# First attention loads in halves, a backlog in the planner, second block's tokens normalised earlier, key differences stored from ScalarE

## The chip, the cores and the metric

The kernel runs on one core of one Trainium2 chip. The time is device microseconds (us) of one execution. The kernel before was timed three times; its median is 1596.62 us (1595.55 to 1596.75).

## The reference

One adaLN transformer block on `x` of shape (2, 1024, 512), all in float32:

```python
mod = (silu(c) @ wmod).reshape(2, 6, 1, 512)      # sa, ca, ga, sb, cb, gb
h = layernorm(x) * (1 + ca) + sa
q, k, v = h @ Wq, h @ Wk, h @ Wv                  # 32 query heads, 8 key heads, 64 wide
q, k = rope(q), rope(k)
attn = softmax(causal(q @ k.T / 8)) @ v           # 4 query heads share a key head
x = x + ga * (attn @ Wo)
h = layernorm(x) * (1 + cb) + sb
gate, up = split(h @ ternary(w_gate_up).T)        # 2048 hidden
x = x + gb * (rmsnorm(silu(gate) * up) @ ternary(w_proj).T)
```

`ternary` replaces each group of 64 weights by -1, 0 or 1 times the mean of their absolute values.

## The kernel before

Products that need float32 accuracy are made of two parts: a value is rounded to `F32R` (the "H" tile, by ScalarE) and what is left over is the "L" tile (`V.tensor_tensor(..., ALU.subtract)` on VectorE). A product is then H·H + L·H + H·L, which is three times the matmuls.

**Stage one, about 0 to 260 us.** The 2048 tokens are four blocks of 512. Each block goes through `keys_values(blk)` and then, for blocks 0 to 2, `queries(blk, g)` for the eight head groups `g`. The order of instructions on each engine is the order of the Python text. `queries` does, for one group: 24 matmuls into two PSUM tiles `pqk` (`rope_mm`); for block 0 the split of another part of Wq (`split_w`, which makes `wqH` on ScalarE and `wqL` on VectorE); four VectorE products with cosine and sine (`ra`, `rc`, `rb`, `rd`, in `rope_mul`) and two sums on GpSimd; and in `rope_end(1)` the split of the group before into `rr`, which SyncE stores to `qs` in DRAM (`put_q`, four transfers of 256 KB). In between, the next block is prepared: `stats` and `rstd` (mean, and the power -1/2 on GpSimd, tile `rs`), `norm` (VectorE, in place in `xt`, two calls in each of the groups 0 and 1), `first_T` (TensorE transposes, tile `pt`, groups 2 to 5) and `first_h` (tiles `h`, `hH`, `hL`).

Keys are stored twice: as values (`ks`), and as differences of keys 128 apart (`kds`, the tiles `ra` and `rc` with their float32r rounding from ScalarE). The SyncE queue issues every transfer of the kernel, in order. Each transfer waits for its source and for the transfer eight before it.

**From block 3's queries on** a planner (`Plan.run`) writes the order. Every step is a task with an engine, an estimated cost, a due time `due`, the tasks it needs, and the buffers and PSUM banks that it takes. The planner keeps its own clock and takes the available task with the smallest due time; its result is a fixed order of instructions for each engine. `moving` is its idea of when the transfers issued so far will have landed, and it starts at 0. The tasks are: 16 halves of the last block's queries (`mm`, 12 matmuls each), attention, the output projection, the second norm, ternary weights (spread between the other stages, the first from `TBEG` before the projection) and the feed-forward.

Attention goes by units: 2 batches x 8 head groups x 4 strips of 256 query rows. For a unit, the row maxima are needed first: `top_mm` (tile `pm`, TensorE), `top_red` (VectorE, tiles `mm` and `mx`), then four small transfers `row<-mt`. The scores (`ps_`), the exponentials (`e`, ScalarE), the weighted values (`po`) and the row sums (`pr`) follow. Tops are due `LEAD` before the unit's scores. `STICK` favours tasks of the kind that TensorE is at, and `FEED`, `BOOST`, `ENOUGH` and `DELAY` move `top_mm` forward or back by how much VectorE has left to reduce.

The first unit of a head group loads its keys: `k1` and `k2` (`load_k`, four transfers of 256 KB), the differences `k3` (`load_steps`, four) and for every second group the values `vt` (`load_v`, 512 KB). Each unit also loads its queries `t` (512 KB). The tiles `rr` of the last queries have two buffers, freed when their four stores have landed:

```python
        ha = add("A", ac(512, 0), due + 8, lambda hi=hi: hi(0, "ra"), (ja,), takes=("rr",))
        w = [add("S", 0.46, due + 11, lambda put=put, h=h: put(h), (la, lc), dma=256 * KB) for h in (0, 2, 1, 3)]
        ha.hold("rr", *w)
```

Of the kernel before, what the change touches and what calls it, by code (L numbers as in the profile page):

```python
# [61 lines left out]
class Plan:  # L62
# [39 lines left out]
    def run(self):  # L102
        wait, then, ready = {}, {}, {}
        for t in self.tasks:
            deps = {d.n: d for d in t.after + t.before}
            wait[t.n] = len(deps)
            for d in deps.values():
                then.setdefault(d.n, []).append(t)
            if not deps:
                ready.setdefault(t.eng, []).append((0.0, t))  # L110
        free, moving, ring, mode, port, left = {}, 0.0, 0.0, 0, 0.0, len(self.tasks)
        rows, owed = [0.0, 0.0], 0.0
        while left:
            best = self.order = None
            for eng, ts in ready.items():
                opts = []
                for r, t in ts:
                    at = self.room(t)
                    if at is not None:
                        now = free.get(eng, 0.0) if eng != "T" else max(rows) if t.lane is None else rows[t.lane]  # L120
                        r = max(r, at, port if eng == "P" or t.mode and eng == "V" else 0.0)
                        opts.append((max(r, now), r > now - AHEAD * (eng == "T"), t))
                if not opts:
                    continue
                start = min(o[0] for o in opts)
# [12 lines left out]
            ready[t.eng] = [o for o in ready[t.eng] if o[1] is not t]  # L138
            self.given = []
            for tag in t.takes:  # L140
                if tag[0] == "#":
                    self.given.append(self.order[len(self.given)][1])
                    self.banks[self.given[-1]] = lambda t=t, tag=tag: t.users[tag]
                else:
                    self.slots[tag].append(lambda t=t, tag=tag: t.users[tag])
            t.emit()
            owed += t.feeds
            if t.eng == "T":
                if t.mode != mode:
                    start = max(start, *rows) + (LEAVE if mode == 0 else ENTER)  # L150
                    rows, mode = [start, start], t.mode
                elif late and t.lane is None:
                    start += LOAD
                t.done = start + t.cost
                if t.lane is None:
                    rows = [t.done, t.done]
                else:
                    rows[t.lane] = t.done
            else:
                free[t.eng] = t.done = start + t.cost  # L160
            if t.eng == "P" or t.mode and t.eng == "V":
                port = t.done + 0.06
            if t.eng is None:
                free[None] = t.done = 0.0
            if t.dma:
                ring = max(start + (0.26 if t.eng == "A" else 0.03), ring) + t.cost
                free[t.eng] = ring
                moving = max(ring + 0.7, moving) + t.dma / 250e3
                t.done = moving + 0.95
            for d in then.get(t.n, ()):  # L170
                wait[d.n] -= 1
                if not wait[d.n]:
                    r = max([a.done + (self.LAG if a.eng != d.eng or a.dma else 0.1) + (SPARE if a.dma and d.eng != "S" else 0.0) for a in d.after], default=0.0)
                    ready.setdefault(d.eng, []).append((r, d))
# [3 lines left out]
EB, EL = 4, 10  # L178
SPAN = {2: 2, 4: 4, 6: 3, 8: 4}
HELD = 4  # L180
TBEG, TEND, PER_UNIT = 300, 20.0, 0.8
VSUM, VSIGN, LAST = 9, 1, 3
TBEFORE, TGAP, TSKIP = 20, 20.0, 25.0
LEAD, SPREAD, STICK, LATE = 15, 0.6, 9, 4
ENTER, LEAVE, LOAD, AHEAD = 0.16, 0.37, 0.1, 0.25
CLASS = (0, 1, 1, 2)
TURN, SPARE = 0.05, 1.0
FEED, BOOST, ENOUGH, DELAY, FILL = 0.3, 22, 2, 8, 3.5
QT, PACE = 6, 4

@with_exitstack
def block_kernel(ctx, tc, x, wq, wk, wv, wo, wgu, wpj, cin, wmod, cos, sin, out):
# [190 lines left out]
    first = {}  # L383
# [77 lines left out]
    def rope_end(n):  # L461
        while len(ropes) > n:
            (a, c, *steps), tok, dst = ropes.pop(0)
            rr = tp.tile([128, 4, 512], F32R, name="rr")
            for i, r in enumerate((a, c)):
# [10 lines left out]
                A.activation(high, steps[i], AF.Copy)  # L476
                V.tensor_tensor(rr[:, 2 + i, 128:512], steps[i], f32(high), ALU.subtract)
                half = [x for pair in kds for x in pair][[x for pair in ks for x in pair].index(dst)][i]
                SY.dma_start(f32(half[:, to:to + 512 - f]), f32(r[:, f:512].bitcast(F32R)))
            for h in (0, 2, 1, 3):  # L480
                if len(dst.shape) == 4:
                    put_q(dst, rr, h, tok)
# [37 lines left out]
    def queries(blk, g):  # L520
        rope_mm(blk, "wq", g * 256, qs[blk // 2][g])
        nxt = blk < 3 and 2 <= g < 6
        if nxt:
            first_T(blk + 1, g - 2)
        if blk == 0 and g < 4:
# [6 lines left out]
            mods_T(g - 1)  # L532
        if nxt:
            first_h(blk + 1, g - 2)
        if blk < 3 and g < 2:
            norm(blk + 1, 2 * g)
            norm(blk + 1, 2 * g + 1)
        rope_end(1)
# [239 lines left out]
    def attention(u):  # L778
# [15 lines left out]
        if u % NI == 0:  # L794
            kd = K[(b, g)] = {}

            def load_k(n):
                l, a = n // 2, n % 2
                if a == 0:
                    kd["k", l] = kp.tile([128, S], F32R, name=("k1", "k2")[l])  # L800
                SY.dma_start(f32(kd["k", l][a * 64:a * 64 + 64, :]), f32(ks[b][g // 4][l * 64:l * 64 + 64, g % 4, :]))

            def load_v():
                kd["vt"] = kp.tile([128, S // 128, 128], F32, name="vt")
                SY.dma_start(kd["vt"], vs[b * S:(b + 1) * S, g * 64:g * 64 + 128].rearrange("(t p) n -> p t n", p=128))

            kd["l"], before = [], K[units[u - 1][:2]]["l"] if u else []
            def load_steps(n):
                if n == 0:
                    kd["k", 2] = pp.tile([128, S // 8 * 7], F32R, name="k3", bufs=2)  # L810
                p = n % 2 * 64 + n // 2 * 32
                SY.dma_start(f32(kd["k", 2][p:p + 32, :]), f32(kds[b][g // 4][n // 2, g % 4 * 32:g % 4 * 32 + 32, :]))

            for n in range(4):
                kd["l"].append(add("S", 0.46, t0 - 26 + n, lambda n=n: load_k(n), order=kd["l"] + (held or before),
                                   takes=(("k1",), (), ("k2",), ())[n], dma=256 * KB))
            for n in range(4):
                kd["l"].append(add("S", 0.46, t0 - 22 + n, lambda n=n: load_steps(n), order=kd["l"], takes=() if n else ("k3",), dma=96 * KB))
            if g % 2 == 0:
                kd["lv"] = add("S", 0.46, t0 - 15, load_v, order=held or (K[units[u - 8][:2]]["lv"],) if u >= 8 else (), takes=("vt",), dma=512 * KB)  # L820
                kd["av"] = []
            else:
                kd["lv"] = K[(b, g - 1)]["lv"]
                kd["av"] = K[(b, g - 1)]["av"]
            kd["use"] = []

        kd = K[(b, g)]

# [40 lines left out]
        for n, (h0, s_, c, lo, hi) in enumerate(jobs):  # L869
            w = (hi - lo) * 128  # L870
            due = t0 - LEAD - pace * (len(jobs) - n)
            m = add("T", pe(w) + 0.03, due, lambda a=(h0, s_, c, lo, hi): top_mm(*a), d["lq"] + kd["l"][:2], takes=("#", "#1"), mode=3)
            tag = "mx" if hi == 2 * i + s_ + 1 else "mm"
            for n_, h in enumerate((h0, h0 + 2)):
                r = add("V", dv(w) + ((0.075 if c else 0.015) if tag == "mx" else 0.0), due + 0.01 * n_, lambda a=(h, s_, c, lo, hi): top_red(*a), (m,), order=[low[h, s_]] if c else (),
# [74 lines left out]
        for at, j in enumerate(order):  # L950
# [1 line left out]
            due = due_s[(u, j)]  # L952
            es[j] = []
            first, c = j in FIRST[nb], max(x for x in FIRST[nb] if x <= j)
            p = add("T", (3 + first) * pe(2 * n) + 0.03, due, lambda j=j: score(j), d["lq"] + kd["l"] + [row] + (cleared[1:2] if u == 0 else []) + ([] if first else es[j - 1]),
                    takes=("#", "#1") if first else (), mode=3)
            if first:
                chain[c] = p
# [15 lines left out]
            if (at + 1) % SPAN[nb] == 0:  # L974
                js = order[at + 1 - SPAN[nb]:at + 1]
                v = add("T", (SPAN[nb] * 2048 - (1024 if nb - 1 in js else 0)) / 2400 + 0.02, due + 5,
                        lambda js=js: [value(x) for x in js], sum((ex[x] for x in js), []) + [kd["lv"]], order=vals[-1:],
                        takes=("#",) if at == SPAN[nb] - 1 else (), mode=1)
                kd["av"].append(v)
                vals.append(v)  # L980
# [645 lines left out]
```

## Time and profile before

| | |
|---|---|
| median of three runs | 1596.62 us |
| profiled execution, its own time | 1598.2 us |
| its span, first to last instruction | 1596.3 us |
| TensorE (PE) busy | 1548.1 us, 97% |
| VectorE (DVE) busy | 1175.4 us, 74% |
| GpSimd (POOL) busy | 863.0 us, 54% |
| ScalarE (ACT) busy | 697.8 us, 44% |
| 16 transfer engines, q1 | 53.0% of their span |
| mean granted TensorE clock | 0.990 |

The profile is one execution of 1598.2 us, 1.6 us above the median, with 1.9 us outside the span. Busy shares are means over stages. TensorE is idle for 48 us in all, so what can be gained lies in where these are. A timeline line gives start, duration, engine, operation, tiles written and read, the count of merged instructions, and in brackets the idle time before and what ended it. `SPq` is SyncE's transfer queue. "L39" is the helper through which every instruction is recorded, so the tiles tell which step a line is.

### The profile page before, as it was taken

The numbers are of one execution on the slowest core, as the hardware profiler recorded it, in microseconds if no ns is written. First come the engines' busy times: TensorE is split into PE (matmuls) and PEld (weight loads), VectorE is DVE, ScalarE is ACT, GpSimd is POOL, SyncE is SP. The second block draws the span as 40 slices with busy tenths as digits, with TensorE's granted clock in tenths as the row PEclk, the third lists the DMA queues.
The fourth block names the chain that finished last, engine by engine and source line by source line (L and its number), as shares of the span: only waits on it lengthen the run. The fifth ranks groups of instructions, "written<-read, shape, count | busy, mean of one in ns | idle before, by whom it ended". The sixth has DMA issues, their size and how long they took to land.

```text
span 1596.3 us, 26757 instructions
## 1 busy us (share of the span) xinstructions
PE 1548.1 (97%) x9028; PEld 1068.0 (67%) x9028; DVE 1175.4 (74%) x2468; ACT 697.8 (44%) x1349; POOL 863.0 (54%) x758
## 2 busy tenths in 40 slices
PE   8899998989999999999999999999999999999998
PEld 7777887745555555555555555477788887888886
DVE  6888887778777788888878888857888674443444
ACT  3322222146555556555555656634655432222221
POOL 4364556537666765765676675713323544444343
PEclk9999999999999999999999999999999999999999
DMA  7775758775555546655646555576777833020000
GB/s 247 243 201 173 225 150 230 227 182 163 154 146 150 143 125 172 167 157 141 169 123 172 146 150 144 161 244 198 251 216 246 288 102 136 1 79 1 11 16 27
DMA packets 206592, 250.55 MB, mean 157 GB/s; under 512 B 34932, under 2 KB 144500, under 8 KB 206456
## 3 DMA queue, kind: packets, MB, share of 16 engines
q1 hardware_dynamic: 206456, 248.85, 53.0%
q8 instruction: 71, 1.16, 0.3%
q14 instruction: 65, 0.53, 0.1%
HBM read 156.24 MB, written 92.02 MB: 156 GB/s over the span
## 4 chain that ended last, share of the span: by engine, by line
PE 70%; DVE 13%; DMA 6%; issue 5%; SPq 3%; ACT 2%; POOL 1%; DVEq 0%; ACTq 0%; POOLq 0%
PE pgu L39 15%; PE po L39 13%; PE pj L39 10%; PE pfo L39 7%; PE pqk L39 6%; PE pm L39 5%; DVE junk L39 3%; SPq L39 3%; PE pr L39 2%; DVE rr L39 2%; DMA k<-ks 1%; DMA t<-qs 1%; DVE mm L39 1%; DVE ra L39 1%; DVE rd L39 1%
## 5 line engine op out<-in xcount | busy, mean ns | idle before, releaser
L39 POOL TENSOR_TENSOR acc<-acc,e 128x512 f32<-128x512 f32 x202 | 266.0, 1328 | 61.6 <-DVE acc L39 47.7
L39 PE MATMUL po<-e,vt 128*64 128x512 f32 (+1 forms) x1280 | 268.0, 557 | 4.2 <-DVE mx L39 1.6
L39 PE MATMUL pgu<-h,gu 128*128 128x512 f32 x1024 | 244.3, 391 | 0.0
L39 PEld LDWEIGHTS pgu<-h,gu 128*128 128x128 f32 x1024 | 192.0, 188 | 39.8
L39 DVE CUSTOM_DVE_ANT_0 junk<-pm,cmask,mm 128x384 bf16<-128x384 f32 (+1 forms) x256 | 174.6, 682 | 57.7 <-PE pm L39 33.2
L39 PEld LDWEIGHTS po<-e,vt 128*64 128x64 f32 x1280 | 84.0, 136 | 154.8 <-issue 123.3
L39 PE MATMUL pm<-k,t 64*128 64x384 f32 (+3 forms) x768 | 167.1, 384 | 16.1 <-DVE mx L39 6.0
L39 POOL TENSOR_SCALAR_AFFINE_SELECT e<-e 128x512 f32<-128x512 f32 x128 | 88.3, 692 | 143.6 <-ACT e L39 140.9
L39 PEld LDWEIGHTS pm<-k,t 64*128 64x128 f32 x768 | 93.5, 185 | 105.6 <-issue 31.6
L39 POOL TENSOR_TENSOR s<-hm 128x512 f32<-128x512 f32 x59 | 68.7, 1164 | 163.3 <-DVE hm L39 163.1
L39 DVE CUSTOM_DVE_ANT_0 junk<-pm,cmask 128x128 bf16<-128x128 f32 (+3 forms) x256 | 124.6, 487 | 41.4 <-PE pm L39 18.8
L39 DVE TENSOR_REDUCE mm<-pm 128x1 f32<-128x384 f32 (+2 forms) x256 | 128.3, 546 | 31.6 <-PE pm L39 31.1
L39 PE MATMUL pj<-woH,oh 128*128 128x512 f32 x512 | 142.2, 399 | 0.0
L39 POOL TENSOR_TENSOR on<-on,ri 128x512 f32<-128x512 f32 x64 | 85.5, 1337 | 66.8 <-DMA ri<-linv 62.7
L39 DVE TENSOR_TENSOR mL<-hm,mH 128x512 fp32r<-128x512 f32 x64 | 75.9, 1186 | 60.7 <-ACT mH L39 60.7
L39 DVE TENSOR_TENSOR hm<-gs,pgu 128x512 f32<-128x512 f32 x64 | 43.9, 686 | 94.3 <-PE pgu L39 89.9
L39 PEld LDWEIGHTS pj<-woH,oh 128*128 128x128 f32 x512 | 95.1, 188 | 20.9 <-issue 2.3
L39 ACT ACTIVATE mH<-hm 128x512 fp32r<-128x512 f32 x64 | 40.4, 632 | 146.1 <-PE pfo L39 133.3
L39 POOL TENSOR_TENSOR ra<-ra,rb 128x512 f32<-128x512 f32 x40 | 51.7, 1291 | 94.4 <-DVE rb L39 82.5
L39 PE MATMUL pfo<-pj,mH 128*128 128x512 f32 x256 | 100.4, 392 | 0.0
L39 PE MATMUL pfo<-pj,mL 128*128 128x512 f32 x256 | 99.7, 389 | 0.0
L39 POOL TENSOR_TENSOR sq<-sq,s 128x512 f32<-128x512 f32 x59 | 80.8, 1369 | 4.5
(1485 smaller groups left out, 3667.6 us busy)
## 6 DMA issues: line engine op xcount, KB each, us to landing
qs<-rr SPq DMA_DIRECT2D x128, 256.0 KB
t<-qs SPq DMA_DIRECT2D x64, 512.0 KB
k<-ks SPq DMA_DIRECT2D x64, 256.0 KB
ri<-linv SPq DMA_DIRECT2D x128, 128.0 KB
os<-on SPq DMA_DIRECT2D x64, 256.0 KB
ks<-rr SPq DMA_DIRECT2D x32, 256.0 KB
w<-in_wgu SPq DMA_DIRECT2D x32, 256.0 KB
gus<-wr SPq DMA_DIRECT2D x32, 256.0 KB
```

Source lines behind the costliest of these rows:

```text
L39: ins = f(*a, **k)
```

## The change

1. `Plan.run` starts `moving` at `BACKLOG` = 8 instead of 0.
2. For the first unit (`u == 0`), `k1`, `k2`, `k3` and `vt` are loaded in two halves each. The first halves keep their due times, the second halves are due from `TSECOND` = 30. Strips 0 and 1 need the first halves alone (`i > 1` adds the rest). That is nine more transfers on SyncE. The size that the planner assumes for a `k3` load goes from 96 to 112 KB.
3. In `queries(0, g)` for `g < 2`, `norm` is called ahead of `split_w`.
4. The stores into `kds` are issued by ScalarE instead of SyncE (16 of them).
5. `TBEG` 300 to 330, `LEAD` 15 to 11, `STICK` 9 to 6, `FEED` 0.3 to 0.6, `BOOST` 22 to 14, `ENOUGH` 2 to 3.

```diff
-        free, moving, ring, mode, port, left = {}, 0.0, 0.0, 0, 0.0, len(self.tasks)
+        free, moving, ring, mode, port, left = {}, BACKLOG, 0.0, 0, 0.0, len(self.tasks)
...
-TBEG, TEND, PER_UNIT = 300, 20.0, 0.8
+TBEG, TEND, PER_UNIT = 330, 20.0, 0.8
...
-LEAD, SPREAD, STICK, LATE = 15, 0.6, 9, 4
+LEAD, SPREAD, STICK, LATE = 11, 0.6, 6, 4
...
-FEED, BOOST, ENOUGH, DELAY, FILL = 0.3, 22, 2, 8, 3.5
+FEED, BOOST, ENOUGH, DELAY, FILL = 0.6, 14, 3, 8, 3.5
+TSECOND, BACKLOG = 30.0, 8.0
...
-                SY.dma_start(f32(half[:, to:to + 512 - f]), f32(r[:, f:512].bitcast(F32R)))
+                A.dma_start(f32(half[:, to:to + 512 - f]), f32(r[:, f:512].bitcast(F32R)))
...
+        if blk == 0 and g < 2:
+            norm(blk + 1, 2 * g)
+            norm(blk + 1, 2 * g + 1)
         if nxt:
             first_T(blk + 1, g - 2)
         if blk == 0 and g < 4:
...
-        if blk < 3 and g < 2:
+        if 0 < blk < 3 and g < 2:
             norm(blk + 1, 2 * g)
             norm(blk + 1, 2 * g + 1)
...
+            parts = 1 + (u == 0)
-            def load_k(n):
+            def load_k(n, part=0):
...
+                c = slice(part * S // parts, (part + 1) * S // parts)
+                SY.dma_start(f32(kd["k", l][a * 64:a * 64 + 64, c]), f32(ks[b][g // 4][l * 64:l * 64 + 64, g % 4, c]))
...
+            if parts == 2:
+                for f, n in [(load_k, 0), (load_k, 1)] + [(load_steps, n) for n in range(4)] + [(load_k, 2), (load_k, 3)]:
+                    kd["m"].append(add("S", 0.46, TSECOND + len(kd["m"]), lambda f=f, n=n: f(n, 1), order=kd["l"] + kd["m"] + [kd["lv"]], dma=(128 if f is load_k else 48) * KB))
+                kd["mv"].append(add("S", 0.46, TSECOND + 8, lambda: load_v(1), order=kd["m"], dma=256 * KB))
...
-            m = add("T", pe(w) + 0.03, due, lambda a=(h0, s_, c, lo, hi): top_mm(*a), d["lq"] + kd["l"][:2], takes=("#", "#1"), mode=3)
+            m = add("T", pe(w) + 0.03, due, lambda a=(h0, s_, c, lo, hi): top_mm(*a), d["lq"] + kd["l"][:2] + kd["m"][:2] * (i > 1), takes=("#", "#1"), mode=3)
```

In the order that results, the changes on TensorE up to the first scores are these: before, 5 query halves of the last block, then the first six `pm` matmuls; after, 8 query halves and then the same six. SyncE's queue at this place, before: nine loads of keys and values with two of `t`, then the stores `qs_0` and `qs_1`, then `row` of unit 0, `qs_2`, `qs_3`, `row` of unit 1, `qs_4`, and `t` of unit 2. After: nine first halves with the two `t`, nine second halves, then `qs_0` to `qs_2`, `row` of unit 0, `qs_3`, `qs_4`, `t` of unit 2, `row` of unit 1. VectorE's order in group 0 of block 0, before: `wqL`, `ra`, `rc`, `rb`, `rd`, `xt`, `xt`; after: `xt`, `xt`, `wqL`, `ra`, `rc`, `rb`, `rd`; and likewise in group 1, whose end has the two `rr` of group 0.

More of the change, by code (lines that the diff above doesn't have):

```diff
@@ L795, in attention @@
             kd = K[(b, g)] = {}
-            def load_k(n):
+            parts = 1 + (u == 0)
+            def load_k(n, part=0):
                 l, a = n // 2, n % 2
-                if a == 0:
+                if a == 0 and part == 0:
                     kd["k", l] = kp.tile([128, S], F32R, name=("k1", "k2")[l])
[L801 to L805, printed above, removed]
+                c = slice(part * S // parts, (part + 1) * S // parts)
+                SY.dma_start(f32(kd["k", l][a * 64:a * 64 + 64, c]), f32(ks[b][g // 4][l * 64:l * 64 + 64, g % 4, c]))
@@ L807, in attention, with load_v, load_steps @@
+            def load_v(part=0):
+                if part == 0:
+                    kd["vt"] = kp.tile([128, S // 128, 128], F32, name="vt")
+                c, r = (slice(part * n // parts, (part + 1) * n // parts) for n in (S // 128, S))
+                SY.dma_start(kd["vt"][:, c], vs[b * S:(b + 1) * S, g * 64:g * 64 + 128][r].rearrange("(t p) n -> p t n", p=128))
             kd["l"], before = [], K[units[u - 1][:2]]["l"] if u else []
-            def load_steps(n):
-                if n == 0:
+            def load_steps(n, part=0):
+                if n == 0 and part == 0:
@@ L810, in load_steps @@
                     kd["k", 2] = pp.tile([128, S // 8 * 7], F32R, name="k3", bufs=2)
                 p = n % 2 * 64 + n // 2 * 32
-                SY.dma_start(f32(kd["k", 2][p:p + 32, :]), f32(kds[b][g // 4][n // 2, g % 4 * 32:g % 4 * 32 + 32, :]))
+                c = (slice(0, S // 8 * 7), slice(0, 512), slice(512, S // 8 * 7))[parts - 1 + part]
+                SY.dma_start(f32(kd["k", 2][p:p + 32, c]), f32(kds[b][g // 4][n // 2, g % 4 * 32:g % 4 * 32 + 32, c]))
             for n in range(4):
@@ L815, in attention @@
                 kd["l"].append(add("S", 0.46, t0 - 26 + n, lambda n=n: load_k(n), order=kd["l"] + (held or before),
-                                   takes=(("k1",), (), ("k2",), ())[n], dma=256 * KB))
+                                   takes=(("k1",), (), ("k2",), ())[n], dma=256 * KB // parts))
             for n in range(4):
-                kd["l"].append(add("S", 0.46, t0 - 22 + n, lambda n=n: load_steps(n), order=kd["l"], takes=() if n else ("k3",), dma=96 * KB))
+                kd["l"].append(add("S", 0.46, t0 - 22 + n, lambda n=n: load_steps(n), order=kd["l"], takes=() if n else ("k3",), dma=112 * KB // parts))
@@ L819, in attention @@
             if g % 2 == 0:
-                kd["lv"] = add("S", 0.46, t0 - 15, load_v, order=held or (K[units[u - 8][:2]]["lv"],) if u >= 8 else (), takes=("vt",), dma=512 * KB)
+                kd["lv"] = add("S", 0.46, t0 - 15, load_v, order=held or (K[units[u - 8][:2]]["lv"],) if u >= 8 else (), takes=("vt",), dma=512 * KB // parts)
                 kd["av"] = []
@@ L825, in attention @@
             kd["use"] = []
+            kd["m"], kd["mv"] = [], K[(b, g - 1)]["mv"] if g % 2 else [kd["lv"]]
+            if parts == 2:
+                for f, n in [(load_k, 0), (load_k, 1)] + [(load_steps, n) for n in range(4)] + [(load_k, 2), (load_k, 3)]:
+                    kd["m"].append(add("S", 0.46, TSECOND + len(kd["m"]), lambda f=f, n=n: f(n, 1), order=kd["l"] + kd["m"] + [kd["lv"]], dma=(128 if f is load_k else 48) * KB))
+                kd["mv"].append(add("S", 0.46, TSECOND + 8, lambda: load_v(1), order=kd["m"], dma=256 * KB))
         kd = K[(b, g)]
@@ L954, in attention @@
             first, c = j in FIRST[nb], max(x for x in FIRST[nb] if x <= j)
-            p = add("T", (3 + first) * pe(2 * n) + 0.03, due, lambda j=j: score(j), d["lq"] + kd["l"] + [row] + (cleared[1:2] if u == 0 else []) + ([] if first else es[j - 1]),
+            p = add("T", (3 + first) * pe(2 * n) + 0.03, due, lambda j=j: score(j), d["lq"] + kd["l"] + kd["m"] * (i > 1) + [row] + (cleared[1:2] if u == 0 else []) + ([] if first else es[j - 1]),
                     takes=("#", "#1") if first else (), mode=3)
@@ L976, in attention @@
                 v = add("T", (SPAN[nb] * 2048 - (1024 if nb - 1 in js else 0)) / 2400 + 0.02, due + 5,
-                        lambda js=js: [value(x) for x in js], sum((ex[x] for x in js), []) + [kd["lv"]], order=vals[-1:],
+                        lambda js=js: [value(x) for x in js], sum((ex[x] for x in js), []) + (kd["mv"] if i > 1 else [kd["lv"]]), order=vals[-1:],
                         takes=("#",) if at == SPAN[nb] - 1 else (), mode=1)
```

## The prediction

> **What bounds the kernel now.** I read the busy shares first, then the waits of TensorE (PE), then windows of 5 us where PE is idle, then timelines of the engine that ends each wait. PE is busy for 97% of the span, so the 48 us that it is not are all there is to gain, plus what a reduced clock takes after a stall.
>
> ```profile
> PE 1548.1 (97%) x9028; PEld 1068.0 (67%) x9028; DVE 1175.4 (74%) x2468; ACT 697.8 (44%) x1349; POOL 863.0 (54%) x758
> PE pt L39 <- DVE xt L39: 6.0, 3, 4.3
> PE pm L39 <- DVE mx L39: 6.0, 19, 0.5
> PE pm L39 <- DMA t<-qs: 5.8, 2, 5.3
> ```
>
> In the waits (total, times, longest) two single waits stand out, and the change is aimed at both: `pt` on `xt` (4.3) and `pm` on the load of `t` (5.3). The rest are waits of half a microsecond on VectorE's maxima. The second one, in windows (PE, PEld, DVE, ACT, POOL busy, clock, transfers) and on PE's timeline:
>
> ```profile
> 270.00:275.00 5.00, 5.00 (x24) 3.98 (x22) 2.99 (x5) 1.00 (x2) 3.80 (x4) 1.00 1.01 292
> 275.00:280.00 5.00, 0.22 (x1) 0.00 (x0) 1.89 (x3) 0.89 (x2) 2.52 (x2) 0.91 1.05 221
> 280.00:285.00 5.00, 4.08 (x12) 3.14 (x13) 2.06 (x12) 0.00 (x0) 0.00 (x0) 0.50 1.09 249
> 280.49 0.44 PE L39 MATMUL pm<-k,t 64*128 64x128 f32 x1 [5.27 <-DMA t<-qs]
> 282.30 2.07 PE L39 MATMUL pqk<-hH,wqH 128*128 128x512 f32 x4
> ```
>
> The transfer engines are full (1.01 to 1.09), PE is empty, and the clock then stands at 0.50, so that four matmuls take 2.07 instead of 1.07.
>
> The first wait, by contrast, is not what sets the time there. VectorE's timeline (DVE), with PE's two lines:
>
> ```profile
> 55.95 2.63 DVE L39 TENSOR_SCALAR xt<-xt,mv,rs 128x512 f32<-128x512 f32 x2
> 64.52 0.68 DVE L39 TENSOR_TENSOR rr<-ra,rr 128x512 fp32r<-128x512 f32 x1
> 65.12 0.68 DVE L39 TENSOR_TENSOR rr<-rc,rr 128x512 fp32r<-128x512 f32 x1
> 97.33 1.47 DVE L39 TENSOR_TENSOR rr<-ra,rr 128x512 fp32r<-128x512 f32 x1
> 98.72 1.78 DVE L39 TENSOR_TENSOR rr<-rc,rr 128x512 fp32r<-128x512 f32 x1
> 63.25 0.33 PE L39 MATMUL pt<-ident,xt 128*128 128x128 f32 x1 [4.28 <-DVE xt L39]
> 113.90 1.19 PE L39 MATMUL pv<-wvH,hH 128*128 128x512 f32 x4 [2.00 <-DVE rd L39]
> ```
>
> From 53 to 114 us VectorE goes from one product to the next, its only gaps being 1.22 us waits on ScalarE's `rr`; at 84.0 (0.36) and 113.9 (2.00) PE waits for it again, for a bank. Time that PE wins at 63 us is waited for at the next bank. What counts up to 113.9 is the length of VectorE's chain.
>
> **The entry to attention (parts 1 and 2): -8.5 us.** From the end of the fifth query half at 275.22 to the `pm` at 315.92, after the last half, 40.7 us pass. In them lie 11 halves of 2.72 (the rows of four start 0.907 apart) and `pm` groups of about 0.5, 0.68 and 0.66: 31.8 us of work. So the stall with its slow clock costs 8.9. After the change three more halves, 3 x 2.72 = 8.2 us, stand ahead of the first `pm`, which moves from 275.2 to 283.4. The query work is only moved forward, so it is free as long as the data is there. Before, `t` was there at 280.49 and the keys at 281.37. In the new order the first keys leave earlier: the two `kds` stores (1.03 + 0.40) that stood in SyncE's way behind `vs` are gone, so the first load goes out at about 270.1 instead of 271.58, and half as many bytes of k1 are needed. The cover is some 3 us. I take 8.5 of the 8.9, since a change between query matmuls and `pm` costs a little each time. Without that cover, the gain falls by what the loads are late.
>
> What is late next is `qs_0`. Nine more transfers stand ahead of it on SyncE. Behind it wait the `rr` buffers of ScalarE (14.44 us until 290.94 in this trace), through them the cosine products, and `t` of unit 2, which now follows `qs_4`. The bytes are the same, and SyncE here is held by the transfer eight before, so the queue moves with the bytes. The two stores that now come later are the same two megabytes that ended the full stretch near 290. I put `qs_0` at 282 to 285 (282.37 before) and price it at nothing; the bounds are 0, and +7 if each of the nine costs SyncE the 0.6 to 0.8 us that its issues show here.
>
> The Trainium skill (DMA: Bandwidth & Descriptors, Rules for kernel authors) speaks against halves: coalesce, because a transfer under 64 KB pays mostly overhead; its section Anatomy of one DMA puts the fixed part at about 2.0 us, for transfers that GpSimd issues. By that, the nine new ones (four of them 48 KB) are an estimated 18 us if nothing overlapped, and the whole gain would be lost. No row of this trace shows halves.
>
> **`norm` ahead of Wq's split (part 3): +1.5 us.** Three things on VectorE's chain. The power that makes `rs` took 1.03 us alone (at 127.21); before, `wqL` lay beside it, now `xt` is next and waits: +1.2 with the hand-over. The first two `xt` then run while GpSimd rests: at 6.65 one took 0.54, against 2.63 for two beside GpSimd's sums at 55.95: -1.6. The two `rr` in group 1, before separated from the sums by `xt` (1.2 for both), now follow the products directly, like those at 97.33 (3.1): +1.9. Sum +1.5, bounds -1.0 (no collision) to +3.1 (the first `xt` stay slow). PE's wait for `xt` gets shorter, and I count that at nothing, for the reason above.
>
> **`kds` from ScalarE (part 4): +2.1 us.** No trace row shows ScalarE issue a transfer. The nearest are SyncE's own `kds` rows:
>
> ```profile
> 35.14 0.33 SPq L39 DMA_DIRECT2D kds<-ra  x1
> 44.07 0.90 SPq L39 DMA_DIRECT2D kds<-ra  x1
> 190.02 0.52 ACT L39 ACTIVATE rc<-rd 128x384 fp32r<-128x384 f32 x1 [1.66 <-DVE rc L39]
> 190.44 0.58 ACT L39 ACTIVATE vt<-pv 128x512 f32<-128x512 f32 x1
> 191.08 1.20 PE L39 MATMUL pv<-wvH,hH 128*128 128x512 f32 x4 [1.01 <-ACT vt L39]
> ```
>
> I take 0.4 each, nearer to the idle queue's 0.33, since the transfers eight before have mostly landed. Behind each stands ScalarE's next rounding, for which VectorE waits, or a copy `vt`, for which PE's bank waits. In block 0 three of four lie on the chain (VectorE waits for `rc`, then for `wqH` at 46.4): +1.2, which reaches 113.9 in full. In block 1 VectorE idles 2.76 us at 118.7; +0.2 is left where it catches PE at 133.4. In block 2 the second one stands ahead of `vt` at 190.44 and the first is half hidden: +0.7. In block 3 PE has free banks: 0. Bounds: 0 if ScalarE pays nothing, +4.7 at 0.90 each. SyncE gains little in blocks 0 to 2, where its next store waited for VectorE anyway.
>
> The skill (same page, Issuing engines are not separate DMA queues) says that a second issuing engine saves only the sequencer's issue time. By it, SyncE is spared four short issues per block and no transfer lands sooner for its own sake; here too no row shows a second issuer.
>
> **The planner's constants (part 5) and the passage to attention: 0, from -6 to +6.** TensorE's instructions are the same in number, and the changes of kind between scores, values and sums are as many in the new order (259 against 261). From 360 to 1040 us PE is idle 16.8 us, and some 12 of these are waits on VectorE of half a microsecond or less; I let a third of that go either way (4). The tops come closer to their scores; the row that shows this was late, `row<-mt`, cost 0.5 once. From 315 to 360 PE idles 5.0 us and the clock loses 3.4 more, which a queue better fed could win back in part, while the rope's remains, if delayed, could add 2.
>
> **Sum.** -8.5 + 1.5 + 2.1 + 0 = -4.9. The profiled execution took 1598.2 (span 1596.3 and 1.9 around it), so its like would take 1593.3; against the median of 1596.62 that is 1591.7.
>
> **Rivals.** (a) *The rope pays nothing and the passage gains.* ScalarE issues for free, the first `xt` offsets the `rr`, and 3 to 4 us return between 315 and 360: -8.5 - 3.5 = -12, 1584 to 1588. For it: the clock of 0.51 at 320 us. Against it: VectorE's chain has no slack. (b) *A new wait takes the place of the old.* The nine second halves hold `qs_0` back by 6 to 7 us; `rr` is released at 297, the rope runs late, and `t` of unit 2 lands at about 315, while PE, with its query work used up, wants it at 309: 6 us of stall and 3 of clock. -8.5 + 3.6 + 9 = +4: 1600 to 1603. It decides once `qs_0` leaves later than about 286. For it: the 14.44 us wait. Against it: the queue is full of bytes, not of issues. (c) *Nothing is left.* Issues at 0.9 and the slow `xt` make the rope cost 7 to 8: 1595 to 1598.
>
> **How the numbers follow.** My forecast, 1588 to 1596, has 0.50, (a) 0.18, (b) 0.20, (c) 0.12. A measurement of this kernel can tell about 0.2%, 3.2 us, from no change. Faster by more than that: 0.42 of the 0.50 and all of (a), 0.60. Within it: 0.08 and 0.09 of (c), 0.17. Slower: (b) and 0.03 of (c), 0.23. The range 1584 to 1601 takes in (a) and the near end of (b).
>
> **What would show it.** Right: no wait of `pm` on `t` or `k` above 1 us near 283, the clock at 1.00 there, the query halves ended 8 us sooner after the last `pv`; yet `pv` of block 1 after 113.9 by 2 to 3 us, with a longer wait on `rd`, and the wait at 191 near 2. Wrong: `pv` at 113.9 or earlier; ScalarE's issues far from 0.4; a wait of `pm` on `t<-qs` or of a score on `row<-mt` after 305; more than 20 us of PE idle in attention.

## The result, and the profile after

The changed kernel is slower: 1607.91 us against 1596.68 us in the same session. The ratio on record is 1.0062, 95% interval 1.0043 to 1.0080 (the two medians alone give 1.0070). The prediction said 1591.7 with a range of 1584 to 1601. The profiled execution took 1608.04 (span 1606.3; before 1598.2 and 1596.3).

The waits of TensorE (total, times, longest) show that both waits the change was aimed at are gone or small, and that others have come:

```profile
PE pm L39 <- DVE mx L39: 5.1, 18, 0.5
PE pqk L39 <- DVE mx L39: 4.6, 1, 4.6
PE pt L39 <- DVE xr L39: 4.4, 4, 2.7
...
PE pt L39 <- DVE xt L39: 2.2, 2, 1.2
```

`pm` on `t` is not in the list, and `pt` on `xt` fell from 6.0 to 2.2. New are 4.6 us in one wait of a query half (`pqk`), and `pt` on `xr` in the second norm, 4.4 where 1.6 were.

**Where the 10 us between the two profiles lie.** I measured both kernels between the same matmuls:

| stretch | before | after | difference |
|---|---|---|---|
| first query half of block 3 starts at | 261.46 | 266.16 | +4.7 |
| from there to the first `pm` of the second head group | 81.4 | 79.5 | -1.9 |
| from there to the first `pj` of the projection | 696.4 | 697.6 | +1.1 |
| from there to the first `pgu` of the feed-forward | 193.1 | 197.9 | +4.8 |
| last `pfo` | 357.3 later | 357.3 later | 0 |
| end of the span | 6.7 later | 7.9 later | +1.2 |

What makes the last 1.2 us is not shown.

*The entry.* Windows of the kernel after, then the timelines of TensorE, ScalarE, VectorE and SyncE's queue in the same stretch:

```profile
285.00:290.00 5.00, 5.00 (x26) 3.87 (x25) 3.03 (x8) 0.00 (x0) 2.11 (x2) 1.00 1.03 228
290.00:295.00 5.00, 5.00 (x25) 3.53 (x24) 1.51 (x10) 0.00 (x0) 1.44 (x2) 1.00 0.82 210
295.00:300.00 5.00, 0.39 (x2) 0.20 (x2) 1.28 (x4) 1.15 (x2) 0.72 (x1) 0.72 0.90 276
300.00:305.00 5.00, 5.00 (x14) 3.70 (x16) 4.71 (x14) 1.15 (x2) 2.69 (x3) 0.60 0.76 209
```

```profile
288.01 0.61 PE L39 MATMUL pm<-k,t 64*128 64x128 f32 x6
...
299.81 2.08 PE L39 MATMUL pqk<-hH,wqH 128*128 128x512 f32 x4 [4.61 <-DVE mx L39]
...
298.06 0.63 ACT L39 ACTIVATE rr<-ra 128x512 fp32r<-128x512 f32 x1 [16.83 <-DMA qs<-rr]
...
298.72 0.69 DVE L39 TENSOR_TENSOR rr<-ra,rr 128x512 fp32r<-128x512 f32 x1 [6.63 <-ACT rr L39]
299.33 0.42 DVE L39 CUSTOM_DVE_ANT_0 junk<-pm,cmask 128x256 bf16<-128x256 f32 x1
299.67 0.08 DVE L39 DVE_READ_ACCUMULATOR2_ANT mx<- 128x1 f32 x1
299.67 0.69 DVE L39 TENSOR_TENSOR ra<-pqk,cs 128x512 f32<-128x512 f32 x1
...
284.83 0.46 SPq L39 DMA_DIRECT2D vt<-vs  x1
...
291.45 12.18 SPq L39 DMA_DIRECT2D qs<-rr  x12
```

At 288.01 `pm` runs without a wait: the data is there, as predicted. But PE then does two more query halves and stops at 295, with an empty window, and the clock falls as it did before. The wait is put down to `mx`, and that row ends at 299.75, 0.06 us before PE goes on: it is the first maximum of the second `pm` group, and a `pm` tile holds its PSUM bank until its maximum is taken. (The cosine product `ra<-pqk` ends later, at 300.36, so it is not what PE waited for.) VectorE's order is fixed, and this maximum stands behind its `rr` at 298.72, which waits for ScalarE's `rr` at 298.06, which waited 16.83 us for a store of `qs`. The stores left at 291.45, behind nine first and nine second halves. The stall was not removed, but moved from the loads to the stores.

*The projection.* GpSimd, VectorE and TensorE around the second norm:

```profile
1112.39 1.41 POOL L39 TENSOR_TENSOR h2L<-h,h2H 128x256 fp32r<-128x256 f32 x2 [3.71 <-issue]
1113.76 0.70 POOL L39 TENSOR_TENSOR rs<-ve,mhalf 128x2 f32<-128x2 f32 x1
...
1114.50 1.94 DVE L39 TENSOR_SCALAR xr<-oacc,mv,rs 128x512 f32<-128x512 f32 x2 [2.29 <-POOL rs L39]
...
1115.59 0.33 PE L39 MATMUL pt<-ident,xr 128*128 128x128 f32 x1 [2.71 <-DVE xr L39]
```

The power `rs` stands behind `h2L` of the token pair before, `xr` waits for it, and PE waits for `xr`. The order has six `pj` matmuls between the two groups of transposes where the kernel before has 18, too few to cover this chain.

### The profile page after: what moved, and what is told of

Read it like the earlier page. It is cut to its first block, busy times and chain, and to the rows that moved or that the text cites. A ratio compares the mean times of both kernels' runs of the same rounds, so it can differ in the third digit from the quotient of the medians.

```text
span 1606.3 us, 26783 instructions
## 1 busy us (share of the span) xinstructions
PE 1551.6 (97%) x9028; PEld 1067.0 (66%) x9028; DVE 1163.5 (72%) x2468; ACT 698.1 (43%) x1349; POOL 859.6 (54%) x758
## 4 chain that ended last, share of the span: by engine, by line
PE 67%; DVE 16%; issue 6%; DMA 6%; ACT 2%; SPq 2%; POOL 1%; ACTq 0%; DVEq 0%; POOLq 0%
PE pgu L39 15%; PE po L39 13%; PE pj L39 10%; PE pfo L39 7%; PE pm L39 4%; DVE junk L39 4%; PE pqk L39 3%; PE pr L39 3%; SPq L39 2%; DVE rr L39 2%; DMA qs<-rr 2%; DVE mm L39 1%; DVE rd L39 1%; DMA t<-qs 1%; DVE ra L39 1%
## 5 line engine op out<-in xcount | busy, mean ns | idle before, releaser
L39 PE MATMUL pm<-k,t 64*128 64x384 f32 (+3 forms) x768 | 170.4, 380 | 10.8 <-DVE mx L39 5.1
L39 ACT ACTIVATE on<-po 128x512 f32<-128x512 f32 x64 | 38.3, 598 | 105.5 <-POOL acc L39 48.9
```

The lines of the kernel that those rows point to most:

```text
L39: ins = f(*a, **k)
```

## The experiments

Fourteen kernels are compared below, each in the same three stretches: stage one from the first to the last start of `pv<-wvL`, the entry from there to the first `pm` of the second head group, and the rest from there to the first `pgu`. After that all are alike, but for the last transfers. Stretches are of one profiled execution each; ratios are of 4 to 12 executions against the kernel before on the same chip. How far single executions differ can be read from the table: the eight kernels whose stage one is that of before take 227.4 to 229.1 for it, and the changed kernel and the one with `kds` back, whose orders are the same from block 3 on, differ by 0.4 in the entry and 3.3 in the rest. Times of single rows are compared below as counted from the first query half of block 3, where that changes the reading.

| kernel | ratio, 95% interval | stage one | entry | rest |
|---|---|---|---|---|
| before | 1 | 228.3 | 81.6 | 889.5 |
| after | 1.0062, 1.0043 to 1.0080 | 234.3 | 79.7 | 895.4 |
| norm alone | 1.0005, 0.9993 to 1.0017 | 229.8 | 80.8 | 888.6 |
| `kds` alone | 1.0022, 1.0008 to 1.0036 | 232.7 | 81.5 | 889.0 |
| constants alone | 1.0091, 1.0070 to 1.0111 | 229.1 | 83.5 | 901.0 |
| halves alone | 1.0049, 1.0031 to 1.0066 | 228.2 | 81.6 | 900.5 |
| after, no halves | 1.0039, 1.0024 to 1.0053 | 233.1 | 78.7 | 892.9 |
| after, `qs_0` ahead of second halves | 1.0061, 1.0040 to 1.0082 | 235.8 | 79.4 | 895.4 |
| after, `kds` back on SyncE | 1.0032, 1.0017 to 1.0047 | 228.5 | 79.3 | 892.1 |
| before, `qs_0` ahead of all loads | 1.0106, 1.0088 to 1.0123 | 227.9 | 77.0 | 912.1 |
| before, `qs_0` and `qs_1` ahead | 1.0069, 1.0054 to 1.0085 | 227.4 | 72.9 | 909.5 |
| the same, four constants set anew | 0.9912, 0.9892 to 0.9933 | 229.0 | 71.9 | 888.9 |
| the same, three other constants | 0.9938, 0.9918 to 0.9959 | 229.0 | 71.2 | 890.4 |
| before, those four constants alone | 1.0064, 1.0042 to 1.0086 | 227.7 | 81.5 | 900.0 |

**Norm alone (part 3 on the kernel before).**

```diff
+        if blk == 0 and g < 2:
+            norm(blk + 1, 2 * g)
+            norm(blk + 1, 2 * g + 1)
...
-        if blk < 3 and g < 2:
+        if 0 < blk < 3 and g < 2:
```

> The kernel before with part 3 alone (norm ahead of Wq's split). The theory is that stage one's edits lengthen VectorE's chain, and that the 4.7 us by which the changed kernel's first query half of block 3 is late (266.16 against 261.46) is the sum of what each costs alone. Then this kernel is 1.5 to 2 us late at pv of block 1 (113.90 before), still 1.5 to 2.5 late at block 3's first query half (263 to 264), and 1598 to 1599 in all. Rival one: PE's shorter wait for xt is kept, pv at 113 or earlier and 1595. Rival two: later waits of block 1 and 2 swallow the delay, pv late but the query half at 261.5 and 1596.7.

Ratio 1.0005: between -1.1 and +2.7 us. Block 1's `pv` starts as before, with the same wait:

```profile
113.84 1.95 PE L39 MATMUL pv<-wvH,hH 128*128 128x512 f32 x4 [1.96 <-DVE rd L39]
```

But this execution's first `pv<-wvL` came 1.5 us sooner than that of the kernel before, so the theory's 1.5 us and nothing at all cannot be told apart here. Block 3's first query half came at 261.38, where the theory asked for 263 to 264. Of the rivals, the one that PE's shorter wait for `xt` is kept has no support; the one that later waits swallow the delay stays open.

**`kds` alone (part 4 on the kernel before).**

```diff
-                SY.dma_start(f32(half[:, to:to + 512 - f]), ...)
+                A.dma_start(f32(half[:, to:to + 512 - f]), ...)
```

> The kernel before with part 4 alone (kds stored from ScalarE). The theory: ScalarE pays some 0.35 us for each issue and 0.40 us more until its next operation, 0.75 in all where the prediction had 0.4, so the edit costs about 0.75 x 2 in block 0, 0.5 to 1 in each of blocks 1 and 2: block 3's first query half at 264 to 264.5 and 1599 in all. Rival one: the issues cost what was predicted, 2.1, 263.5 and 1598.7. Rival two: they are hidden here and cost only beside the moved norm: 261.5 and 1596.7.

Stage one is 4.3 us longer; the changed kernel's is 5.9 longer. ScalarE's timeline in block 1, of the kernel before and then of this one, followed by this one's waits on PE:

```profile
121.48 0.53 ACT L39 ACTIVATE ra<-rb 128x384 fp32r<-128x384 f32 x1
121.91 0.62 ACT L39 ACTIVATE rr<-rc 128x512 fp32r<-128x512 f32 x1
```

```profile
124.29 0.53 ACT L39 ACTIVATE ra<-rb 128x384 fp32r<-128x384 f32 x1
124.85 0.33 ACTq L39 DMA_DIRECT2D kds<-ra  x1
125.22 0.63 ACT L39 ACTIVATE rr<-rc 128x512 fp32r<-128x512 f32 x1 [0.40 <-ACT ra L39]
...
115.86 1.20 PE L39 MATMUL pv<-wvH,hH 128*128 128x512 f32 x4 [2.01 <-DVE rd L39]
120.49 1.21 PE L39 MATMUL pv<-wvH,hH 128*128 128x512 f32 x4 [1.61 <-ACT vt L39]
127.51 1.20 PE L39 MATMUL pqk<-hH,wqH 128*128 128x512 f32 x4 [1.25 <-ACT vt L39]
195.42 1.20 PE L39 MATMUL pv<-wvH,hH 128*128 128x512 f32 x4 [1.53 <-ACT vt L39]
```

Before, the next rounding starts 0.43 us after `ra<-rb`; with the issue between them, 0.93. The issue starts when its source is complete, and the next operation when the issue is done: +0.50 each (two of the 16 issues were 0.57 and 0.59 long, the others 0.33 or 0.34). That is less than the theory's 0.75, yet the first query half came at 266.08, later than its 264 to 264.5, since PE pays at 115.86 (+1.96 against 113.90) and then twice in block 1 for `vt`, where I had put 0.2 us. The rival "hidden here" falls.

**Constants alone (part 5 on the kernel before).**

```diff
-TBEG 300, LEAD 15, STICK 9, FEED 0.3, BOOST 22, ENOUGH 2
+TBEG 330, LEAD 11, STICK 6, FEED 0.6, BOOST 14, ENOUGH 3
```

> The kernel before with part 5 alone (the six constants). Its order already has three more query halves ahead of the first pm, with the loads whole, and the second norm's two transpose groups are 18 pj matmuls apart as before (6 in the changed kernel). The theory says that the stall at 280 needs only the three query halves, and that the wait of 4.6 us at 300 comes from the nine second halves ahead of qs_0: then qs_0 leaves at 282 to 283, PE has no wait above 1 us between 275 and 316, the last query half ends 7 to 8 us earlier, the projection takes what it took before, and the total is 1588 to 1591. Rival one: the stall moves to the wait at 300 here too, since the bytes ahead of qs_0 are the same: 1596 to 1598. Rival two: the constants themselves lose in attention and projection: above 1600.

1.0091: the theory of that moment fell, and this run showed the mechanism. Here the loads are whole, eight query halves stand ahead of `pm`, and `qs_0` leaves at 279.73: 19.9 us after the first query half, where it was 25.3 in the changed kernel and 20.9 before. PE stalls all the same:

```profile
279.73 19.56 SPq L39 DMA_DIRECT2D qs<-rr  x16
...
289.23 0.63 ACT L39 ACTIVATE rr<-ra 128x512 fp32r<-128x512 f32 x1 [14.38 <-DMA qs<-rr]
...
289.89 0.69 DVE L39 TENSOR_TENSOR rr<-ra,rr 128x512 fp32r<-128x512 f32 x1 [9.58 <-ACT rr L39]
...
291.10 0.68 DVE L39 TENSOR_TENSOR rd<-pqk,cs 128x512 f32<-128x512 f32 x1
...
291.84 2.80 PE L39 MATMUL pm<-k,t 64*128 64x256 f32 x6 [6.62 <-DVE rd L39]
```

Here PE waits for a cosine product (`rd`, done at 291.78), which stands behind VectorE's `rr` as the maximum did in the changed kernel. The third `rr` is written at 289.23. Counted from the first query half that is 29.4 us, in the kernel before 29.5, in the changed one 31.9. PE can do nine or ten query halves before it needs that: here it stopped after nine, in the changed kernel after ten. Five halves and a stall of 5.27 us, or eight and a stall of 6.62, come to the same buffer at the same time. So second halves are not needed for the new wait. Rival two holds as well: attention and projection took 11.5 us more than before.

**Halves alone (part 2 on the kernel before; `moving` starts at 0).**

```diff
+            parts = 1 + (u == 0)
```

> The kernel before with the halves alone (old constants, no backlog, kds from SyncE). PE's order up to the first scores is that of before: five query halves, then pm. The theory now: between 262 and 290 us the transfer engines are full, and PE's query work goes no further than the two rr buffers allow, which are freed when the stores of qs_0 and qs_1 have landed. Halves move no byte away from ahead of qs_0, so the wait of pm on t shrinks from 5.3 to some 3, but rr is released no earlier than the 290.94 of before (291 to 294), and the query halves end within 1.5 us of before: 1596 to 1599. Rival (the prediction's step): first halves remove the stall, -4 to -6: 1591 to 1593.

The query rows of this kernel:

```profile
279.16 1.50 PE L39 MATMUL pm<-k,t 64*128 64x128 f32 x6 [3.26 <-DMA t<-qs]
...
293.13 0.63 ACT L39 ACTIVATE rr<-ra 128x512 fp32r<-128x512 f32 x1 [15.95 <-DMA qs<-rr]
```

The first halves make the wait 2 us shorter, and `rr` comes 2.2 us later than before (1.5 counted from the first query half); the query halves end 53.2 us after the last `pv<-wvL` (54.8 before), and the entry is as long as before, 81.6. The theory's 3 us and 291 to 294 were right, its total was not, with a ratio that stands for some 1604.5: the order that the planner then makes loses 11 us in the rest.

**After, without the halves.**

```diff
-            parts = 1 + (u == 0)
+            parts = 1
```

> The changed kernel without the halves (parts = 1), all else kept. Its order has eight query halves ahead of pm, and the second norm's two transpose groups 6 pj matmuls apart as in the changed kernel. The theory: stage one +4.7, an entry in which PE waits 5 to 7 us for the rope near 290 with the slow clock behind it, as with the constants alone, attention +2 to +5, projection +4 to +5 for the 6 matmuls: 1608 to 1613. Rival one: the second halves are what hold qs_0 back, then the entry wins 4 to 6 against the changed kernel and it takes 1602 to 1604. Rival two: the projection's loss is not the spacing, then pj to pgu takes 193 as before where the changed kernel has 198.

1.0039 against 1.0062: the difference is 0.2%, 4 us, but the two intervals overlap, so that halves cost time is not shown. The total missed the theory's 1608 to 1613; it is some 1603, which rival one named, but the entry gained 1.0 us against the changed kernel and not rival one's 4 to 6. The wait is 2.94 us instead of 4.61 (3.60 in the kernel with `kds` back, which has the halves):

```profile
298.04 1.95 PE L39 MATMUL pqk<-hH,wqH 128*128 128x512 f32 x4 [2.94 <-DVE mx L39]
```

The projection again has its 2.71 us wait, and `pj` to `pgu` takes 198.6 us, so rival two falls.

**After, `qs_0` ahead of the second halves.**

```diff
-... order=kd["l"] + kd["m"] + [kd["lv"]], ...
+... order=kd["l"] + kd["m"] + [kd["lv"]] + qputs[0], ...
```

> The changed kernel with one edit: the second halves wait for the stores of qs_0, so SyncE's queue has qs_0 ahead of them. In the order that results the second norm's two transpose groups stand 30 pj matmuls apart (6 in the changed kernel). The theory: qs_0 leaves at 286 to 287 where it left at 291.45, PE's wait of 4.61 at 300 and the slow clock behind it go (-4 to -6), and the projection gets back to its old length (-4 to -5): 1597 to 1600. Rival one: the wait at 300 is VectorE's work on the maxima and stays: only the projection comes back, 1603. Rival two: second halves that come later hold back the tops of unit 2: 1605 or more.

Half right. `qs_0` leaves at 286.42, the third `rr` is there at 293.09 instead of 298.06 (25.4 us after the first query half instead of 31.9), and the wait is 2.57 us instead of 4.61. The projection is back (193.2 us with 30 matmuls between the groups). But the total is as before the edit, not the theory's 1597 to 1600: the new order lost 4.6 us in attention, what the projection gave. Rival two's total came; whether its reason, later tops of unit 2, is the cause is not shown.

**After, `kds` back on SyncE.**

```diff
-                A.dma_start(f32(half[:, to:to + 512 - f]), ...)
+                SY.dma_start(f32(half[:, to:to + 512 - f]), ...)
```

> The changed kernel with part 4 alone taken back (kds from SyncE again); every engine's order from block 3's queries on is the same. The theory: stage one returns to the length of before (first query half at 261 to 262 instead of 266.2), what follows keeps its length, 1603 to 1604 against 1608. Rival one: the entry is bound by transfers, and an earlier end of stage one only waits there: 1606 to 1608. Rival two: the moved norm costs in this kernel what it did not alone, 1605 to 1606.

The order of every engine from block 3's queries on stays. 1.0032 against 1.0062: 4.8 us, near the 4.3 that `kds` alone had added to stage one. The first query half came at 261.21. The theory holds; both rivals' totals lie outside the interval.

**The stores ahead of the loads.** If the buffer `rr` is what binds, its stores have to go first, though not a byte less is moved. On the kernel before, without any part of the change:

```diff
-        held = qputs[min(2 * u, KVH - 1)] if 2 <= u < 12 else []
+        held = qputs[min(2 * u, KVH - 1)] if 2 <= u < 12 else qputs[0] if u == 0 else []
```

> The kernel before with one edit: the first unit's loads of keys, values and queries wait for the stores of qs_0, and qs_1 goes out between the keys and their differences. Nine query halves then stand ahead of the first pm (five before). No byte is moved away. The theory: rr is freed early (its third use near 280 instead of 290.94), nine halves cover the loads until 286, PE has no wait above 2 us between 262 and 300, the clock stays at 1.00 there and the query halves end 5 to 8 us earlier: 1589 to 1593. Rival one: the bytes set the time whatever their order, the loads land at 290 or later, and pm waits 4 to 6 us there: 1595 to 1598. Rival two: later tops hold back the first scores and lose it again: above 1598.

and with `qputs[1]`, both stores ahead:

> As the one with qs_0 ahead of the first unit's loads, but with qs_0 and qs_1 both ahead, and eleven query halves before the first pm. The theory: rr is free for the third and fourth group, and the fifth group waits for qs_2, which now stands behind eight of the loads: a wait on the rope of 2 to 4 us near 290 is left, 1591 to 1595. Rival one: eleven halves reach further than the loads, no wait at all, 1588 to 1591. Rival two: VectorE gets the maxima of the first units late and in a bunch, and PE waits for them between 305 and 330: 1597 or more.

Both totals missed. With one store ahead the entry did what the theory said, with two what rival one said. Counted from the last start of `pv<-wvL`, the query halves end after 47.9 us with one store ahead and after 47.5 with two (54.8 before). With one, `pm` waits 4.50 us for `t` at 313, after the queries, and the entry keeps 4.6 us of the gain; with two, rival one holds, no wait above 1 us, and it keeps 8.7. But the rest takes 910 to 912 us instead of 889.5. The waits of the second of these, near the end of attention and in the projection, say where some 12 of these us lie:

```profile
PE pq L39 <- ACT wabs L39: 8.8, 3, 5.2
PE pr L39 <- POOL acc L39: 3.7, 1, 3.7
```

The planner's constants were set for another order. With four of them set anew:

```diff
-TBEG 300, LEAD 15, STICK 9, DELAY 8
+TBEG 330, LEAD 9, STICK 4, DELAY 5
```

> The kernel with qs_0 and qs_1 ahead of the first unit's loads, with four constants set anew for the order that this makes (TBEG 330, LEAD 9, STICK 4, DELAY 5), so that the second norm's transpose groups are 18 and 36 pj matmuls apart as in the kernel before. The theory: reordering the stores wins the entry (6.9 us less of PE idle time and slow clock than before), and the loss of 22 us at attention's end (pq waiting 8.8 for wabs, pr 3.7 for acc) came only from constants that no longer fit the order: 1588 to 1592 here. Rival one: the loss at the end belongs to the earlier entry, since the work left for the end stays the same: 1600 to 1606. Rival two: other constants cost attention 4 to 6, 1594 to 1598.

0.9912: 1583.09 us against 1596.87, faster than both kernels and than the theory's 1588 to 1592. Its entry, in windows and timelines:

```profile
280.00:285.00 5.00, 5.00 (x24) 4.14 (x23) 2.73 (x5) 0.90 (x2) 4.19 (x3) 1.00 0.92 213
285.00:290.00 5.00, 5.00 (x23) 3.81 (x21) 2.74 (x6) 0.63 (x1) 3.81 (x3) 1.00 1.03 228
290.00:295.00 5.00, 4.24 (x24) 3.09 (x23) 4.17 (x18) 0.00 (x0) 0.96 (x2) 1.00 1.08 288
```

```profile
271.13 8.57 SPq L39 DMA_DIRECT2D qs<-rr  x8
...
279.11 0.64 ACT L39 ACTIVATE rr<-ra 128x512 fp32r<-128x512 f32 x1 [4.34 <-DMA qs<-rr]
...
289.73 0.96 PE L39 MATMUL pm<-k,t 64*128 64x128 f32 x6
...
294.66 0.62 PE L39 MATMUL pm<-k,t 64*128 64x384 f32 x4 [0.70 <-DMA t<-qs]
```

The transfer engines are as full as before (0.92 to 1.08), PE has no empty window, the clock stays at 1.00, and the third `rr` is written at 279.11, 11.8 us sooner (10.1 counted from the first query half). The waits for `wabs` and `acc` are gone. Of the 12.0 us between the two profiles, 9.7 lie in the entry; 2.4 lie ahead of the first `pv<-wvL`, where kernels with the same stage one differ as much.

With another set:

```diff
-LEAD 15, STICK 9, BOOST 22
+LEAD 11, STICK 6, BOOST 14
```

> As the one before it, with another set (LEAD 11, STICK 6, BOOST 14; TBEG and DELAY as in the kernel before), whose order has the same entry and the same spacing in the second norm. The theory: the entry wins the same 6 to 7, and the two differ by less than 3 us: 1589 to 1594. Rival: the result hangs on the constants by chance, and the two differ by 5 or more.

0.9938, nearly the same entry, and a little faster than the theory's 1589 to 1594. The two sets are 4.2 us apart by the ratios, and their intervals overlap, so whether they differ by less than 3 us or by 5 stays open. And the control, the first set without the stores' new place:

> The control for the fastest one so far: the kernel before with its four constants (TBEG 330, LEAD 9, STICK 4, DELAY 5), but with the first unit's loads where they were, ahead of qs_0. Five query halves stand ahead of pm as in the kernel before. The theory says that the gain comes from the stores' place: the entry loses some 13 us of PE time here as in the kernel before (4.4 in the fastest), and the time is 1596 to 1603. Rival: the constants alone make the gain, 1583 to 1588.

1.0064, slower than the theory's 1596 to 1603, with the old entry, 81.5 against 81.6:

```profile
280.40 0.44 PE L39 MATMUL pm<-k,t 64*128 64x128 f32 x1 [5.29 <-DMA t<-qs]
...
292.58 0.63 ACT L39 ACTIVATE rr<-ra 128x512 fp32r<-128x512 f32 x1 [16.18 <-DMA qs<-rr]
```

So the gain of 9.7 us in the entry comes from the place of the stores, with the eleven query halves that the planner then puts ahead of `pm`; more halves alone do not make it, as the kernel with the constants alone shows (eight, entry 83.5). The constants only keep the rest from losing it, and they do so in this order alone: with the stores in their old place the rest takes 900.0. A third `rr` buffer, which would test the buffer without moving a transfer, was not run.

## Why the prediction was wrong, step by step

**The step that failed** is in the first term, "The query work is only moved forward, so it is free as long as the data is there". It needs more than data: each group of two halves takes one of two `rr` buffers, and these come free with the stores of `qs`, not with PE. Behind a late `rr` stand VectorE's next cosine products and maxima, and with them the PSUM banks that PE needs. The trace of before showed this row (`rr` at 290.94 after 14.44 us), and the prediction named it, but read it as what would be late next if `qs_0` were delayed. It was already the limit: without any delay PE has work for nine or ten halves. The term of -8.5 measured -1.9 in the changed kernel, -2.9 without the halves, and +1.9 with the constants alone; the last two have no second halves ahead of `qs_0`.

Of the 14.8 us between the forecast (-4.9) and the profiles (+9.9), 6.6 lie in this term, 5.9 in attention and projection, 1.1 in stage one (+4.7 for a forecast of +3.6) and 1.2 at the end.

**`qs_0` priced at nothing** failed too. It left at 291.45; less the 4.7 by which stage one is late, this is 286.8, past the point (286) at which rival (b) was said to decide, and 4.4 later than before; `rr` was released 2.4 later than before, counted in the same way. The first load went out 0.6 later, and not 1.5 sooner. Rival (b) is near to what happened: 6.6 us pass from the last first half to `qs_0`, 1.0 before. Its place was wrong: PE stopped at the query halves at 295, not at `t` of unit 2 at 309. Its price, 6 us of stall and 3 of clock, measured 4.61 and, from the rows of four that took 2.08, 1.91 and 1.37 instead of 1.07, some 2.2.

**The halves against the skill.** A small transfer's fixed part did not add up nine times here. Nine second halves went out between 285.57 and 291.45, 0.65 us each. The comparison puts their cost between nothing and some 7.5 us (an estimate from the two intervals). The estimate of 18 us from the Trainium skill (DMA: Bandwidth & Descriptors, Anatomy of one DMA) is for no overlap, and the runs lie far below it; whether halves cost anything is not shown.

**`kds`, +2.1: right in kind, mis-sized.** It measured +4.3 in stage one and 4.8 us in the comparison with this part taken back. Each issue cost 0.50, not 0.4, and block 1, given 0.2, paid about 1.9. Two issues there stood ahead of each `vt` that PE waited for, at 120.49 and 127.51.

**`norm`, +1.5: neither shown nor refuted.** The rows were as predicted (`xt` at 54.08 after 1.14 us of waiting for `rs`, the two `rr` in group 1 at 1.44 and 1.78), and PE's time won at 63 was waited for again at 71.28 (2.69, on `rd`). Alone it costs between -1.1 and +2.7. The two kernels that have it without `kds` took 229.8 and 228.5 in stage one, those without either 227.4 to 229.1.

**The constants, 0 within 6.** The bound was too narrow: all kernels whose planner had other input or other constants, the changed one among them and but for the two that were set anew, took 892 to 912 us in the rest, the kernel before 889.5. The prediction counted TensorE's kinds of work in the new order, and not the distance between a chain's start and its user, such as the six matmuls between two groups of transposes. The projection took 196.3 to 198.6 in the three kernels with six, and 193.1 before; it took 202 to 204 in three others with 12 or 18, mainly for other waits, so the spacing is one cause among several. This distance could be read from the order before the run.

**Signs given in advance.** At 288, which is 283 in the time of the kernel before, there was no wait of `pm` and the clock stood at 1.00; `pv` of block 1 came 1.86 later, though its wait on `rd` stayed 2.00; the wait at 191 was 1.55. The one sign that bore on the sum, query halves ended 8 us sooner after the last `pv`, measured 1.4. None of the signs listed as wrong came: a query half waiting for the rope's bank was not among them.

## What to carry to other kernels

Before moving work forward into a stall, list every buffer that this work takes and ask when each comes free; a stall on a load and a stall on a store can end at the same time, and then filling one only shows the other. Where the transfer engines are full, order can be worth more than size: send first the transfer that frees a buffer the busiest engine needs, and let loads that wait behind work in hand come later. And constants of a planner belong to one order: judge an edit of its input with the constants set anew, or its effect is hidden by the loss elsewhere (here 1.0069 against 0.9912 with entries of 72.9 and 71.9).

## What was not expected of the hardware

- A transfer issued by ScalarE in the middle of its work holds it for 0.50 us: 0.33 for the issue, and the rest because it starts only when the operation before has ended and the next one starts only behind it (0.93 from start to start instead of 0.43).
- From the first store of `qs_0` leaving SyncE to the release of its buffer, 6.6 to 9.9 us passed in this full stretch (291.45 to 298.06 in the changed kernel, 271.13 to 279.11 in the fastest, 279.73 to 289.23 with the constants alone, 286.37 to 296.29 without halves), for 1 MB.
- Profiles of the same stage one differ by 3 us and more at the start: in the eight kernels that share it the first `pv<-wvL` begins between 30.5 and 33.7 us, and in one of them at 37.2. Stretches of single profiles are to be taken between two matmuls, not from the start.
